# A two-layer Mamba and MLP block on one core: scan tiles of 16 channels by 8 states instead of 8 by 16

## The chip, the cores and the metric

The kernel runs on one core of a Trainium2 chip. The metric is the device time of one execution in microseconds, as a median of runs. The profile page shows one profiled execution; its engines are PE (matmul), PEld (weight load), DVE (VectorE), ACT (ScalarE), POOL (GpSimd), and SP, which here only issues DMAs.

## The reference, cut to what matters

Input x is (8 images, 64, 64, 96) in float32. Layer 0 is a visual state-space block. Per image, after group normalisation and a projection, a depthwise 3x3 convolution and SiLU give u, 192 channels by L = 4096 positions. Four scans (k = 0..3) run over it: row order, column order, and both reversed.

```python
dts, Bs, Cs = split(x_proj_w[k] @ u_k)          # 6, 16 and 16 rows, each L long
delta = softplus(dt_proj_w[k] @ dts + dt_proj_b[k])
def step(h, inp):                               # h: (192 channels, 16 states)
    ul, dl, Bl, Cl = inp
    dA = exp(dl[..., None] * A)
    h = dA * h + (dl * ul)[..., None] * Bl[:, :, None, :]
    y = einsum('bkdn,bkn->bkd', h, Cl)
    return (h, y)
```

The four results are summed in row-major order, normalised, gated with SiLU(z), projected back to 96 channels and added to x. Layer 1 upsamples by two with a band-limited filter, applies a 96-384-96 MLP with a quadratic activation, filters, downsamples and adds.

## The kernel before

**The main stream.** For each image the four directions run in the order k = 1, 0, 2, 3, and each in NCH = 4 chunks of T = 1024 positions. A chunk has NT = 24 tiles of 128 partitions by 1024 positions: 8 channels by 16 states each. The program is written as one loop over all 3072 tiles (8 x 4 x 4 x 24, L1207). In step i it places, on in-order engines:

- `fetch` of tile i + 6 (L1070): SP issues one DMA that broadcasts 8 rows of du = delta * u from DRAM over the 16 states, 512 KB, into one of 4 buffers `dub`;
- `product_c` of tile i - 1 if that tile belongs to POOL (every third one, `by_pool`);
- `product_b` of tile i + 3 (L1078): POOL multiplies dub by `br`, the broadcast of B, into one of 4 buffers `bb`;
- `decay` of tile i + 1 (L1082): six bf16 matmuls on PE copy delta (in three bf16 parts) to the 128 partitions, and ACT applies exp with the scale `neg_a`;
- `scan` of tile i (L1097) on DVE, then `product_c` by `cr`, the broadcast of C, on DVE unless the tile is POOL's, and `hold` (L1118), which keeps the last column in `carry`;
- `sums` (L1132), every second step: matmuls with `sel_r` add the 16 states of a channel.

`LEAD, FETCH = 3, 6` (L1184) are the distances. For each chunk `prepare` (L956) loads u, projects it to xd (rows for delta, C and B), broadcasts B and C from SBUF in halves of 256 KB, and computes delta and du, which goes to DRAM in 6 transfers. POOL multiplies delta by u there (L1040). It runs about one chunk ahead.

**The side work.** Everything else is cut into generators that yield what the next piece needs of each engine. `Side.advance` (L109) runs once a step: each active generator moves one piece if the allowance per step (`CAPS`, L50) has it. `front` (L516) of the next image does normalisation, convolution and the gate z. There `conv` (L573) computes blocks of 8 columns and ACT copies each, transposed, into `xt` (L592), which holds the whole image; `lay` (L601) writes it to DRAM in row order once all blocks are done, in rows of 2 KB per channel or pieces of 128 bytes. `tail` (L648) of the image before loads the sum of the row-order directions as a whole table `ye` (L657), then per block of 8 columns loads `ty` (column-order sum) and `tz` (gate); POOL adds (L687), PE, ACT and DVE normalise, gate and project. `mlp` (L783) is layer 1, with `up_h`, `rows_` and `down_h`; its tiles `t1s`, `t1r`, `xu`, `mq` rotate in few buffers. SP issues all transfers on one queue, in the order of the program, and stands when an earlier one must wait for its buffer or its data.

After the last tile the last image's tail and MLP are drained with nothing beside them.

Of the kernel before, what the change touches and what calls it, by code (L numbers as in the profile page):

```python
# [18 lines left out]
HF = 2  # L19
Q3 = 3  # L20
NS = 16
R = 6
K = 4
# [15 lines left out]
class Side:  # L39
# [10 lines left out]
    CAPS = dict(pe=(2.5, 3.2), act=(2.3, 3.0), dve=(1.5, 1.5), pool=(1.4, 2.7), dma=(270, 450))  # L50
# [87 lines left out]
def kernel(ctx: ExitStack, tc: tile.TileContext, a: dict, out: bass.AP):  # L138
# [32 lines left out]
    for p in range(2):  # L171
# [21 lines left out]
    neg_a = cp.tile([128, K, NT], F32, name="neg_a")  # L193
    queue().dma_start(
        neg_a.rearrange("p k g -> p (k g)"),
        a["a_logs"].rearrange("(c n) k f q j -> n c (k f q j)", n=NS),
    )

    sel_r = cp.tile([128, 4, 32], F32, name="sel_r")
    queue().dma_start(  # L200
        sel_r.rearrange("p j m -> p (j m)"), a["sel_r"].rearrange("(c n) j m -> n c (j m)", n=NS)
    )

    sel_b = cp.tile([128, 8, NS, 8], BF16, name="sel_b")
# [68 lines left out]
    def constants_in():  # L273
        nc.gpsimd.memset(xp, 0.0)
        raw["sel"] = tile_([128, 8, 128], "sel_0")
# [20 lines left out]
    def constants_of_scans():  # L296
        yield {}

        nc.scalar.activation(neg_a, neg_a, AF.Exp)
        nc.vector.tensor_scalar(neg_a, neg_a, -1.0, None, ALU.mult)  # L300
        nc.vector.tensor_copy(sel_b, raw["sel"].rearrange("p j (c n) -> p j n c", n=NS))
# [214 lines left out]
    def front(b):  # L516
# [6 lines left out]
        def begin():  # L523
# [6 lines left out]
            v["xt"] = [bp.tile([128, H, w], F32, tag=f"xt{w}", name=f"xt{w}", bufs=1) for w in (W, W // 2)]  # L530
# [3 lines left out]
        def piece(g):  # L534
# [3 lines left out]
            t = bp.tile([128, 4, C], F32, tag="x", name="x", bufs=4)  # L538
# [34 lines left out]
        def conv(n, g):  # L573
# [5 lines left out]
            for tap in range(9):  # L579
# [11 lines left out]
            xt = v["xt"][n]  # L591
            nc.scalar.copy(  # L592
                xt[:, :, 8 * g : 8 * g + 8].rearrange("p h w -> p w h"), e.rearrange("p (i j) -> p i j", i=8)
            )
            for rows, cs, blk in parts_of(n, g):
                filtered.add((b, n, blk))
                nc.sync.dma_start(
                    u_dram[b][1][cs, MB * blk : MB * blk + MB], e[rows]
                )

        def lay(n):  # L601

            yield {}
            while not all((b, n, blk) in filtered for blk in range(8)):
                yield {}
            for h0 in range(0, H, 8):
                yield dict(dma=262 if n == 0 else 131)
                h1 = h0 + 8
                if n == 0:
                    src = v["xt"][0][:, h0:h1].rearrange("p h w -> p (h w)")  # L610
                    nc.sync.dma_start(u_dram[b][0][0:128, W * h0 : W * h1], src)
                else:
                    u = u_dram[b][0][128:192].rearrange("c (h w) -> c h w", h=H)
                    for p in range(2):
                        nc.sync.dma_start(u[:, h0:h1, 32 * p : 32 * p + 32], v["xt"][1][64 * p : 64 * p + 64, h0:h1])
            yield {}
            laid.add((b, n))
# [21 lines left out]
        lays = [(4, 0, lambda n=n: lay(n)) for n in range(2)]  # L639
# [4 lines left out]
        if b == 0:  # L644
            return start + convs[:4], convs[4:] + lays + gates + [bp.close(), bp.close()]
        return start, convs + lays + gates + [bp.close()]

    def tail(b, keep, pairs=True):  # L648
# [3 lines left out]
        def begin():  # L652
# [4 lines left out]
            v["ye"] = [bp.tile([C, H, W], F32, tag=f"ye{f}", name=f"ye{f}", bufs=1) for f in range(HF)]  # L657
            for h0 in range(0, H, 8):
                for f in range(HF):
                    yield dict(dma=200)  # L660
                    nc.sync.dma_start(
                        v["ye"][f][:, h0 : h0 + 8].rearrange("p h w -> p (h w)"),
                        y_dram[b][0][f * C : f * C + C, W * h0 : W * h0 + 8 * W],
                    )
            yield {}
            yield {}

        def block(g):
# [6 lines left out]
            for t, src in zip(yz, (y_dram[b][1], z_dram[b])):  # L675
                for f in range(HF):
# [3 lines left out]
                    )  # L680
# [686 lines left out]
```

## Time and profile before

| | |
|---|---|
| median of 3 runs | 10,879.19 us (10,876.58 to 10,884.08) |
| profiled execution, its own time | 10,889.88 us |
| span in the profile, granted PE clock | 10,888.1 us, 0.977 |
| first scan starts, last scan ends | 139.2 us, 10,612.8 us |
| POOL: products by B / by C / u | 7183.5 / 2423.0 / 491.7 us |
| DVE: scans (four groups) / products by C | 7159.9 / 2508.7 us |

The page gives the busy time of each engine and, for groups of instructions, what ended the idle time ahead of them. Durations overlap by some tens of ns where instructions follow each other, so work per tile is read from one start to the next.

### The profile page before, as it was taken

Reading aid. Unit: us, or ns where it says so; the run is one execution under the profiler, and the core shown is the slowest. Engines: PE = TensorE matmul, PEld = TensorE weight load, DVE = VectorE, ACT = ScalarE, POOL = GpSimd, SP = SyncE. Lnnn points to the kernel's source line nnn. Section 1 sums busy time; section 2 is a strip of 40 time slices with the busy share of each in tenths; the row PEclk is TensorE's granted clock in tenths of the full one; section 3 lists DMA queues with packets and bytes.
Section 4 is the critical chain, followed back from the end, with each engine's and each line's share of the span. In section 5 each row is a group of like instructions: output and inputs, shape, how many; then the busy total and the mean of one; then the engine's idle time right before and its main releaser. Section 6 shows DMA issues by size and latency. Waiting matters only on the chain. (4 is left out here: it accounts for less than half of the span.)

```text
span 10888.1 us, 152912 instructions
## 1 busy us (share of the span) xinstructions
PE 9406.6 (86%) x52498; PEld 3129.1 (29%) x52498; DVE 9965.6 (92%) x7319; ACT 6891.4 (63%) x10138; POOL 10172.5 (93%) x4674
## 2 busy tenths in 40 slices
PE   7788778988789988899889997898978989789888
PEld 2222222422233222332223322233222432223325
DVE  5999999999999999999999999999999999999990
ACT  5666556767567665666656666566756767566653
POOL 4999999999999999999999999999999999999990
PEclk8999999999999999999999999999999999999998
DMA  6879898898988989898998989899898898988981
GB/s 155 224 200 234 218 236 216 221 235 232 239 214 225 235 233 233 214 225 232 240 228 220 230 223 247 217 225 234 231 237 218 222 232 234 239 214 223 230 207 49
DMA packets 1052725, 2402.30 MB, mean 221 GB/s; under 512 B 302012, under 2 KB 322748, under 8 KB 1051944
## 3 DMA queue, kind: packets, MB, share of 16 engines
q1 hardware_dynamic: 1050968, 2391.48, 87.0%
q8 instruction: 413, 6.77, 0.3%
q14 instruction: 368, 3.01, 0.1%
q10 hardware_dynamic: 976, 1.04, 0.0%
HBM read 1929.05 MB, written 328.73 MB: 207 GB/s over the span
## 5 line engine op out<-in xcount | busy, mean ns | idle before, releaser
L1080 POOL TENSOR_TENSOR bb<-dub,br 128x1024 f32<-128x1024 f32 x3072 | 7183.5, 2367 | 149.2 <-DMA dub<-du 95.6
L1095 ACT ACTIVATE pd<-pd,neg_a 128x1024 f32<-128x1024 f32 x3072 | 3339.4, 1087 | 3051.3 <-PE pd L1087 3026.1
L1102 DVE TENSOR_TENSOR_SCAN pd<-pd,carry,bb 128x1024 f32<-128x1024 f32 x1536 | 3605.4, 2347 | 279.3 <-ACT pd L1095 162.6
L1087 PE MATMUL pd<-dp,sel_b 64*128 64x512 bf16 x18432 | 2596.7, 385 | 1075.4 <-DVE carry L1122 686.6
L1108 DVE TENSOR_TENSOR hc<-pd,cr 128x1024 f32<-128x1024 f32 x2048 | 2508.7, 1225 | 144.8 <-PE py L1141 3.2
L1108 POOL TENSOR_TENSOR hc<-h,cr 128x1024 f32<-128x1024 f32 x1024 | 2423.0, 2366 | 180.3 <-DVE h L1102 151.4
L1102 DVE TENSOR_TENSOR_SCAN h<-pd,carry,bb 128x1024 f32<-128x1024 f32 x768 | 1797.5, 2341 | 1.7 <-ACT pd L1095 1.6
L1141 PE MATMUL py<-hc,sel_r 128*32 128x512 f32 x12288 | 1736.0, 620 | 48.6 <-POOL hc L1108 47.1
L1087 PEld LDWEIGHTS <-sel_b 64*128 64x128 bf16 x18432 | 722.7, 94 | 3602.7 <-issue 1557.1
L1102 DVE TENSOR_TENSOR_SCAN pd<-pd,bb 128x1024 f32<-128x1024 f32 x512 | 1173.3, 2292 | 128.2 <-ACT carry L1122 52.2
L565 PE MATMUL pc<-pad,convr 96*128 96x512 f32 (+1 forms) x2304 | 844.0, 610 | 2.1 <-issue 2.1
L1115 PE MATMUL idle<-xp,ident 128*128 128x384 f32 x1450 | 662.9, 540 | 3.2 <-ACT t1s L807 3.2
L1102 DVE TENSOR_TENSOR_SCAN h<-pd,bb 128x1024 f32<-128x1024 f32 x256 | 583.7, 2280 | 14.8 <-ACT pd L1095 11.6
L1040 POOL TENSOR_TENSOR u<-dl,u 128x512 f32<-128x512 f32 x384 | 491.7, 1280 | 108.7 <-ACT dl L1035 108.7
L1017 PE MATMUL pv<-xd,dt_w 64*64 64x512 f32 x1536 | 425.4, 632 | 166.9 <-ACT xd L994 164.5
L1141 PEld LDWEIGHTS py<-hc,sel_r 128*32 128x32 f32 x12288 | 253.4, 109 | 977.2 <-issue 751.4
L859 PEld LDWEIGHTS p<-w2q,mq 128*100 128x100 f32 x4800 | 461.9, 168 | 169.3 <-issue 135.2
L852 PE MATMUL ph<-xu,w 96*128 96x500 f32 x960 | 493.6, 617 | 16.0 <-ACT xu L846 9.2
L859 PE MATMUL p<-w2q,mq 128*100 128x96 f32 x4800 | 504.2, 256 | 2.3 <-ACT mq L853 2.3
L1032 PE MATMUL pv<-e,ident 128*128 128x512 f32 x768 | 437.1, 651 | 27.9 <-ACT pv L1030 27.0
L1042 ACT CAST dp<-pv 128x512 bf16<-128x512 f32 x768 | 452.1, 589 | 5.0 <-PE pv L1041 5.0
L984 PE MATMUL px<-u,xp 64*64 64x512 f32 x1536 | 417.2, 618 | 5.1 <-DMA u<-u 3.2
(162 smaller groups left out, 8195.4 us busy)
## 6 DMA issues: line engine op xcount, KB each, us to landing
dub<-du SPq DMA_DIRECT2D x3072, 512.0 KB
u<-u SPq DMA_DIRECT2D x768, 128.0 KB
du<-u SPq DMA_DIRECT2D x768, 128.0 KB
y<-yq SPq DMA_DIRECT2D x768, 128.0 KB
br<-xd SPq DMA_DIRECT2D x256, 256.0 KB
cr<-xd SPq DMA_DIRECT2D x256, 256.0 KB
yp<-y SPq DMA_DIRECT2D x384, 128.0 KB
yp<-u SPq DMA_DIRECT2D x192, 128.0 KB
```

The source lines that it names most:

```text
L565: nc.tensor.matmul(t[rows].rearrange("p (i j) -> p i j", i=8), weights[:, cs], v["pad"][:, 8 * blk + kw : 8 * blk + kw + 8, kh : kh + H], ...
L852: nc.tensor.matmul(t[:, :px], w1[:, m, :], xu, start=True, stop=True)
L859: nc.tensor.matmul(t[:SIDE, C * i : C * i + C], sq[:, m, row], w2q[:, m, :], start=(m == 0), stop=(m == 2))
L1040: nc.gpsimd.tensor_tensor(v["u"][:, q, :], dl, v["u"][:, q, :], ALU.mult)
L1042: nc.scalar.copy(dp[:, p, :], t)
L1080: nc.gpsimd.tensor_tensor(t["bb"], t["dub"], t["got"]["br"], ALU.mult)
L1087: nc.tensor.matmul(pd[:, MB * hf : MB * hf + MB], sel_b[rows, 4 * t["s"] + t["j"]].rearrange("p n c -> p (n c)"), t["got"]["dp", t["q"]][r ...
L1095: nc.scalar.activation(pd, pd, AF.Exp, scale=neg_a[:, t["k"], t["g"] : t["g"] + 1])
L1102: nc.vector.tensor_tensor_scan(t["h"][:, ::step], pd[:, ::step], t["bb"][:, ::step], 0.0 if t["first"] else held, ALU.mult, ALU.add)
L1108: (nc.gpsimd if t["by_pool"] else nc.vector).tensor_tensor(t["hc"], t["h"], t["got"]["cr"], ALU.mult)
L1115: nc.tensor.matmul(p, ident, xp[:, 0:2].rearrange("p k q r -> p (k q r)"), start=True, stop=True)
L1141: nc.tensor.matmul(py[r0 : r0 + 32], sel_r[:, t["j"], :], t["hc"][:, MB * hf : MB * hf + MB], start=(t["j"] == 0), stop=(t["j"] == 3 and t ...
```

## The change

A tile is now 16 channels by 8 states. Two tiles (i and i + 2) hold the lower and upper 8 states of the same 16 channels and share one `dub`, fetched once; `FETCH` is 7. The product by B stays one instruction per tile. B and C go to DRAM (`bc`) and come back as broadcasts of 8 states each, two for B (one tile `br` of two halves) and two for C (three rotating tiles `cr`; the second half of the next chunk's C is fetched in the last step of a chunk). `xt` becomes three rotating tiles of 16 columns, which are written out as soon as two neighbouring blocks are done, in pieces of 16 elements (64 bytes). The table `ye` is loaded per two blocks, 16 columns at a time, also in pieces of 64 bytes. Several side buffers are fewer, and the allowance of DMA per step is larger.

```diff
-    CAPS = dict(pe=(2.5, 3.2), act=(2.3, 3.0), dve=(1.5, 1.5), pool=(1.4, 2.7), dma=(270, 450))
+    CAPS = dict(pe=(2.5, 3.2), act=(2.3, 3.0), dve=(1.5, 1.5), pool=(1.4, 2.7), dma=(450, 700))
...
-    neg_a = cp.tile([128, K, NT], F32, name="neg_a")
...
+    neg_a = cp.tile([128, 2, K * NT // 2], F32, name="neg_a")
+    sel_r = cp.tile([128, 2, 32], F32, name="sel_r")
...
+    sel_b = cp.tile([128, 4, 128], BF16, name="sel_b")
...
-            t = bp.tile([128, 4, C], F32, tag="x", name="x", bufs=4)
+            t = bp.tile([128, 4, C], F32, tag="x", name="x", bufs=3)
...
-            xt = v["xt"][n]
+            two = (n, g // 2)
+            if two not in v:
+                v[two] = bp.tile([128, H, 16], F32, tag="xt", name="xt", bufs=3)
...
+            v[n, "done"] = v.get((n, "done"), ()) + (g,)
+            if g ^ 1 in v[n, "done"]:
+                side.stores.append([l := lay(n, g // 2), next(l)])
+
+        def lay(n, two):
+
+            yield {}
+            xt, u = v[n, two], u_dram[b][0].rearrange("c (h w) -> c h w", h=H)
+            for h0 in range(0, H, 16):
+                yield dict(dma=131)
+                h = slice(h0, h0 + 16)
+                for rows, cs, blk in parts_of(n, 2 * two):
+                    nc.sync.dma_start(u[cs, h, 8 * blk : 8 * blk + 16], xt[rows, h, :])
...
-            v["ye"] = [bp.tile([C, H, W], F32, tag=f"ye{f}", name=f"ye{f}", bufs=1) for f in range(HF)]
-            for h0 in range(0, H, 8):
-                for f in range(HF):
-                    yield dict(dma=200)
-                    nc.sync.dma_start(
-                        v["ye"][f][:, h0 : h0 + 8].rearrange("p h w -> p (h w)"),
-                        y_dram[b][0][f * C : f * C + C, W * h0 : W * h0 + 8 * W],
-                    )
...
+            if ("ye", g // 2) not in v:
+                ye = v["ye", g // 2] = bp.tile([C, HF, H, 16], F32, tag="ye", name="ye", bufs=2)
+                for f in range(HF):
+                    src = y_dram[b][0][f * C : f * C + C].rearrange("c (h w) -> c h w", h=H)
+                    for h0 in range(0, H, 32):
+                        yield dict(dma=200)
+                        nc.sync.dma_start(
+                            ye[:, f, h0 : h0 + 32, :], src[:, h0 : h0 + 32, 16 * (g // 2) : 16 * (g // 2) + 16]
+                        )
...
-                s.append(bp.tile([SIDE, MB], F32, tag="t1s", name="t1s", bufs=5))
+                s.append(bp.tile([SIDE, MB], F32, tag="t1s", name="t1s", bufs=4))
...
-            s = v[r0] = bp.tile([128, 5, C], F32, tag="t1r", name="t1r", bufs=4)
+            s = v[r0] = bp.tile([128, 5, C], F32, tag="t1r", name="t1r", bufs=3)
...
-            xu = bp.tile([C, px], F32, tag="xu", name="xu", bufs=4)
+            xu = bp.tile([C, px], F32, tag="xu", name="xu", bufs=3)
...
-                    sq = bp.tile([128, 3, px], F32, tag="mq", name="mq", bufs=3)
+                sq.append(bp.tile([128, px], F32, tag="mq", name="mq", bufs=6))
...
+    def repeat(got, name, half):
+
+        if name == "cr":
+            t = got[name, half] = pp.tile([128, T], F32, tag=name, name=name, bufs=3)
+        else:
+            if half == 0:
+                got[name] = pp.tile([128, 2, T], F32, tag=name, name=name)
+            t = got[name][:, half, :]
+        r0 = NS * (name == "br") + 8 * half
+        nc.sync.dma_start(t, got["bc"][None, r0 : r0 + 8, :].to_broadcast([NS, 8, T]))
...
-            for name, row in (("br", 48), ("cr", 32)):
-                t = got[name] = pp.tile([128, T], F32, tag=name, name=name)
-                for hf in range(2):
-                    yield dict(dma=256)
-                    src = xd[64 * hf + row : 64 * hf + row + NS, None, :]
-                    nc.sync.dma_start(t[:, MB * hf : MB * hf + MB], src.to_broadcast([NS, 8, MB]))
+            bc = got["bc"] = dr.tile([2 * NS, T], F32, tag="bc", name="bc")
+            yield dict(dma=128)
+            for hf in range(2):
+                nc.sync.dma_start(bc[:, MB * hf : MB * hf + MB], v["xd"][64 * hf + 32 : 64 * hf + 64, :])
+            yield {}
+            yield {}
+            for name, half in (("br", 0), ("br", 1), ("cr", 0), ("cr", 1))[: 4 if first else 3]:
+                yield dict(dma=512)
+                repeat(got, name, half)
...
-    def fetch(t):
-        assert t["got"].get("ready", 0) > t["q"]
-        t["dub"] = sp.tile([128, T], F32, tag="dub", name="dub", bufs=4)
-        g = t["g"]
-        nc.sync.dma_start(
-            t["dub"], t["got"]["du"][None, 8 * g : 8 * g + 8, :].to_broadcast([NS, 8, T])
-        )
+    def fetch(m):
+
+        t = tiles[m]
+        assert t["half"] == 0 and t["got"].get("ready", 0) > t["q"]
+        t["dub"] = tiles[m + 2]["dub"] = sp.tile([128, T], F32, tag="dub", name="dub", bufs=4)
+        r0 = 64 * t["q"] + 32 * t["s"] + 8 * t["j"]
+        nc.sync.dma_start(t["dub"], t["got"]["du"][r0 : r0 + 16, None, :].to_broadcast([16, 8, T]))
...
-        nc.gpsimd.tensor_tensor(t["bb"], t["dub"], t["got"]["br"], ALU.mult)
+        nc.gpsimd.tensor_tensor(t["bb"], t["dub"], t["got"]["br"][:, t["half"], :], ALU.mult)
+
+    def fetches(i):
+
+        if i % 4 < 2 and 0 <= i < len(tiles):
+            fetch(i)
...
-    LEAD, FETCH = 3, 6
+    LEAD, FETCH = 3, 7
...
-            if i + FETCH < n:
-                fetch(tiles[i + FETCH])
+            fetches(i + FETCH)
+            if i % NT == NT - 1 and i + 1 < n:
+                repeat(tiles[i + 1]["got"], "cr", 1)
```

## The prediction

> **What bounds the kernel now.** I read the page first: its busy line, the DMA line and the costliest groups.
>
> ```profile
> span 10888.1 us, 152912 instructions
> PE 9406.6 (86%) x52498; PEld 3129.1 (29%) x52498; DVE 9965.6 (92%) x7319; ACT 6891.4 (63%) x10138; POOL 10172.5 (93%) x4674
> DMA packets 1052725, 2402.30 MB, mean 221 GB/s; under 512 B 302012, under 2 KB 322748, under 8 KB 1051944
> q1 hardware_dynamic: 1050968, 2391.48, 87.0%
> L1080 POOL TENSOR_TENSOR bb<-dub,br 128x1024 f32<-128x1024 f32 x3072 | 7183.5, 2367 | 149.2 <-DMA dub<-du 95.6
> L1102 DVE TENSOR_TENSOR_SCAN pd<-pd,carry,bb 128x1024 f32<-128x1024 f32 x1536 | 3605.4, 2347 | 279.3 <-ACT pd L1095 162.6
> L1108 POOL TENSOR_TENSOR hc<-h,cr 128x1024 f32<-128x1024 f32 x1024 | 2423.0, 2366 | 180.3 <-DVE h L1102 151.4
> ```
>
> POOL and DVE are both full, and the DMA engines are not far behind. How full the two are per tile is in the timeline of each, start to start (three products in a row are one line of the first view):
>
> ```profile
> 5012.47 1.26 POOL L1040 TENSOR_TENSOR u<-dl,u 128x512 f32<-128x512 f32 x1
> 5013.70 4.67 POOL L1080 TENSOR_TENSOR bb<-dub,br 128x1024 f32<-128x1024 f32 x2
> 5018.33 2.34 POOL L1108 TENSOR_TENSOR hc<-h,cr 128x1024 f32<-128x1024 f32 x1
> ...
> 5000.41 2.35 DVE L1102 TENSOR_TENSOR_SCAN pd<-pd,carry,bb 128x1024 f32<-128x1024 f32 x1
> 5003.94 2.34 DVE L1102 TENSOR_TENSOR_SCAN h<-pd,carry,bb 128x1024 f32<-128x1024 f32 x1
> 5006.36 2.36 DVE L1102 TENSOR_TENSOR_SCAN pd<-pd,carry,bb 128x1024 f32<-128x1024 f32 x1
> ```
>
> A POOL product is (5018.33 - 5013.70) / 2 = 2.31 us, a u product 1.23. A chunk of 24 tiles has 24 products by B, 8 by C and 3 u products: 32 x 2.31 + 3 x 1.23 = 77.6 us. On DVE a scan with its product by C takes 5003.94 - 5000.41 = 3.53 us and a scan for POOL 2.42, so three tiles take 9.48 and a chunk 75.8. Everything else in a chunk can add to the time only by waits, or by side work on these two engines. The windows of four chunks of one image (us, busy per engine, PE clock, DMA share, GB/s):
>
> ```profile
> 5442.00:5529.80 87.80, 70.46 (x342) 18.08 (x334) 79.47 (x63) 48.83 (x74) 84.94 (x40) 1.00 1.02 249
> 5704.60:5792.70 88.10, 71.80 (x398) 21.70 (x390) 78.43 (x64) 51.28 (x81) 79.04 (x38) 0.87 0.79 210
> 5949.40:6026.30 76.90, 73.89 (x489) 31.46 (x488) 74.21 (x41) 56.36 (x80) 76.90 (x36) 1.00 0.90 223
> 6184.70:6265.00 80.30, 68.30 (x416) 24.86 (x412) 78.06 (x62) 51.00 (x81) 74.79 (x34) 1.00 0.99 243
> ```
>
> The third runs at POOL's own 77 us although DMA is 90% busy: loaded DMA engines alone cost nothing. The others lose time. The chain of waits names what for:
>
> ```profile
> POOL hc L1108 <- DVE h L1102: 151.4, 160, 7.3
> DVE pd L1102 <- ACT pd L1095: 202.8, 246, 2.8
> DVE pd L1102 <- ACT carry L1122: 119.1, 148, 3.7
> POOL bb L1080 <- DMA dub<-du: 95.6, 86, 6.1
> DVE pd L1102 <- POOL bb L1080: 72.3, 32, 25.3
> ACT t1s L807 <- DMA t<-t1s: 68.2, 51, 4.3
> SPq L1074 <- POOL bb L1080: 3636.4, 1861, 7.0
> ```
>
> Of POOL's waits only 95.6 us are for a broadcast of du that has not landed (89.5 of them after the first chunk). The last line is why: SP stands a third of the time before a fetch whose buffer POOL still reads, so a fetch leaves three tiles ahead of its use, and all other transfers stand behind it.
>
> **The change, part by part.**
>
> *Broadcasts of du.* 3072 DMAs of 512 KB become 1536. The packet records by size give 393,344 packets of 4 KB with a mean of 258 ns, 6340 us on each of 16 engines; half, 3170, goes. B and C take 512 DMAs of 512 KB where there were 512 of 256 KB: 65,536 packets at 258 for 123 ns (the 2 KB mean), +552 us; the detour of B and C through DRAM adds 8192 packets of 2 KB, +63. In the built order the buffer of the fetch of tiles 8 and 10 is free after the product of tile 2, so a fetch now leaves five products (5 x 3.3 = 16.5 us) ahead of its use in place of three (10 us). The longest wait of before was 6.1 us, so the wait on dub goes: between 0 and -95.6 us. Where DVE is the fuller engine the time doesn't come back whole (the fourth window: POOL loses 5.5 us, but DVE has 78.06 busy), and 89.5 is the part in the loop. I take -80, near the upper end, since in the waiting chunks both engines show holes.
>
> *Engines.* Products, scans, exponentials and matmuls keep number and shape; PE loads one of 4 selections where there were 8. 0 us. Start to start, POOL's product is 2.314 us with DMA under 30% busy and 2.313 at over 90%, so a lighter DMA doesn't quicken it.
>
> *Side work earlier.* The table of even rows, 16 transfers ahead of the tail, is no longer loaded up front, and the DMA allowance per tile rises from 270 to 450. In the built order the tail's first addition on POOL stands at tile 401 of the stream where it stood at 420 (image 1 starts at 384), and DVE's side work of a chunk is more bunched (3 and 9 gates in two chunks where it was 8 and 4; 4, 4, 4 convolutions where it was 2, 4, 4, 2). With 0.70 us for each DVE piece and 1.5 for each addition, the sum over 128 chunks of the larger of 75.8 + DVE's and 77.6 + POOL's is 10,224 us before and 10,248 after: +24. Bounds: 0, as three tiles of lead smooth it, and +48.
>
> *Pieces of 64 bytes.* Laying out u takes 393,216 stores of 64 bytes, where it had 65,536 of 128 bytes and 8192 of 2 KB; reading the even rows takes 393,216 loads where it had 12,288 of 2 KB. The nearest rows: 64-byte loads of constants took 10.4 ns each, 128-byte stores 13.4, 384-byte ones 31.5 in the mean. By the first the new pieces cost 511 us of the engines, by the last 1549, for 213 removed. The queue's 87.0% (9473 us) becomes (9473 - 3170 + 552 + 63 - 213 + 511) / 10888 = 66%, or 76%. That hides them in the mean, not in a burst: two blocks issue 8 loads of 3072 pieces in four tiles (13.4 us), twice per image. At 10.4 ns one is 3072 x 10.4 / 16 = 2.0 us and the eight 16; with 2 fetches (4.1) and other loads (some 5) the backlog is 25 - 13.4 = 12 us, under the 16.5 of the lead: 0. At 31.5 ns one is 6.0, the backlog 44 us and the wait 27 us, 16 times: +430. I take 0, as the 64-byte row is the same size and direction. POOL's addition of the even rows now waits on these loads, three pauses (10 us) behind the last issue; behind it stand the products by B. The same backlog covers it.
>
> The Trainium skill ("DMA: Bandwidth & Descriptors", Specifications) speaks against these pieces: it asks for at least 512 bytes for line rate and says that below it the engine reads, modifies and writes. No run here shows what that costs at 64 bytes; the 10.4 and 13.4 ns above show no jump. If it did make a piece as dear as the 384-byte row, the sum would be the +430 case.
>
> *Smaller buffers.* t1s 4 for 5, t1r 3 for 4, xu 3 for 4, mq 6 for 9, x 3 for 4, xt in three parts. The copy to t1s already waits 68.2 us for its transfer; a buffer less adds, the freer queue takes off. Bounds: -32 us (what DVE and POOL lost behind it) and +32; 0. The order of the last image's MLP on PE is unchanged, so its 240 us of PE in the last 288 us stay.
>
> *Ends.* In the last image the even rows of the last two blocks are now fetched behind their other loads. POOL waited 9.0 us there for ty; four more issues (0.6 each) and 4 x 2.0 us come on top of it: between +4 (overlapping issue) and +26 (6.0 each); I take +7. At the start, writing B and C out and reading them back, and 5 more issues of constants, lie beside the convolutions (PE is busy from 68.8 to 110 us, while SP idles): +3, between 0 and +8.
>
> Sum: -80 + 24 + 0 + 0 + 7 + 3 = -46. The profiled execution took 10,889.9 us (span 10,888.1); it lies 10.7 above the median of 10,879.2. So 10,843.9 against the profile, **10,833** as a median.
>
> **The rivals.** A difference under 0.2% (22 us: 10,857 to 10,901) is about what a measurement cannot tell from none.
>
> 1. *The small pieces clog the queue (slower).* The place is the burst of 8 loads at the start of each image. It decides above some 13 ns per piece, where the backlog passes the lead. For it: 384-byte pieces cost 31.5, and the fastest burst of 128-byte stores (1024 in 1.18 us on 16 engines) makes 18.5 each. Against it: the constants at 10.4. At 18.5 one load is 3.55 us, the backlog 24, less 16.5: 8 us, 16 times, +128: 10,833 + 128 + 8 in the tail = 10,969.
> 2. *The waits only change their name (same).* DVE is as full as POOL; its waits for ACT and POOL's for DVE (322 and 151 us) don't come from DMA. If half of the 80 comes back: 10,873.
> 3. *The freer queue does more.* The ACT wait for t1s goes too (-32), and bunching costs nothing (-24): 10,777; with 32 of DVE's 72.3 us of waits for POOL's product gone as well, 10,745.
>
> **How the numbers follow.** Forecast (10,780 to 10,857): 0.52. Rival 1: 0.22. Rival 2: 0.16. Rival 3: 0.10. Faster is the forecast and rival 3, 0.62; same 0.16; slower 0.22. The range goes from 10,745 to 10,940: it leaves out the dearer part of rival 1 (0.12) and little below. Faster cases alone: 10,745 to 10,857.
>
> **What would show it.** Right: POOL's wait for dub falls from 95.6 to under 15 us, SP's wait for POOL to a small part of 3636, q1 at 64 to 70%, products still 2.31 us apart, the chunk with DMA waits 3 to 5 us shorter. Wrong: dub or the even rows still named behind POOL's idle time, a DMA share near 1 at the start of each image, q1 above 76%; or POOL's and DVE's waits for each other and for ACT growing by as much as dub's shrink.

## The result

The changed kernel took 10,895.63 us (median, 10,879.09 to 10,906.54) beside 10,879.46 us (10,863.63 to 10,906.51) for the kernel before, run beside it. The ratio is 1.0014, with a 95% interval of 1.0007 to 1.0020: 15 us, or 0.14%, slower. By the bound of 0.2% that is "the same"; the forecast was 46 us faster.

The page of the changed kernel, with the rows that answer to those of before (busy line, DMA line, queue, and three groups with busy time, mean ns, and idle time by releaser):

```profile
span 10896.6 us, 149147 instructions
PE 9467.0 (87%) x52574; PEld 3148.1 (29%) x52574; DVE 9965.9 (91%) x7319; ACT 6875.2 (63%) x10139; POOL 10172.9 (93%) x4674
DMA packets 1545527, 1747.69 MB, mean 160 GB/s; under 512 B 1003868, under 2 KB 1024476, under 8 KB 1544776
q1 hardware_dynamic: 1543800, 1737.14, 67.0%
L1100 POOL TENSOR_TENSOR bb<-dub,br 128x1024 f32<-128x1024 f32 x3072 | 7179.2, 2365 | 65.0 <-DVE pd L1131 49.8 <-DMA dub<-du 10.1 <-DVE h L1131 1.9
L1137 POOL TENSOR_TENSOR hc<-h,cr 128x1024 f32<-128x1024 f32 x1024 | 2420.4, 2364 | 236.4 <-DVE h L1131 176.1 <-PE px L1004 33.1 <-PE pd L1116 9.9
```

The queue fell from 87.0% to 67.0%, as worked out (66%). POOL's wait for dub fell from 95.6 to 10.1 us. POOL is as busy as before and the time did not fall, so POOL lost elsewhere what it gained here. The waits of the whole run (total, times, longest) show where, the last two lines for SP's queue:

```profile
POOL hc L1137 <- DVE h L1131: 176.1, 179, 6.5
DVE pd L1131 <- ACT pd L1124: 163.2, 232, 2.1
DVE pd L1131 <- ACT carry L1151: 123.2, 155, 6.4
POOL bb L1100 <- DVE pd L1131: 49.8, 77, 2.3
POOL ty L696 <- DMA ye<-y: 34.0, 5, 20.8
SPq L1096 <- POOL bb L1100: 2250.2, 894, 12.2
SPq L1066 <- POOL u L1062: 1284.1, 347, 13.3
```

POOL waits 25 us longer for DVE's h (151.4 before), and 34 us for the even rows, which had no wait on this list; 22.9 of the 34 are in the end. The last row of the page names a third place: 33.1 us put down to PE's px, the projection of a later chunk. Before, that was

```profile
POOL hc L1108 <- PE px L984: 9.2, 7, 1.8
```

DVE's wait for ACT's exponentials, in contrast, fell from 202.8 to 163.2 us. SP still stands 3534 us for POOL; the second line is the store of du behind the u product.

I cut the profiled time into three parts, from DVE's timeline: the start (up to the first scan), the loop (first scan's start to the last scan's end), and the end (from there to the end of the span). Parts in this document are cut so, one profiled execution each. Such an execution can lie well off the median of its kernel (10.7 us above it for the kernel before, 17 below it for the sharing alone further down), so differences under some 20 us are not resolved by the parts.

| | start | loop | end |
|---|---|---|---|
| before | 139.2 | 10,473.6 | 275.3 |
| changed | 141.2 | 10,456.9 | 298.5 |
| difference | +2 | -17 | +23 |

So the loop gained 17 us where 56 (80 less 24) were forecast, and the end lost 23 where 7 were. The rest of this part is the search for both.

### The profile page after: what moved, and what is told of

Same layout as the page of the kernel before. It is cut to its first block, busy times and chain, and to the rows that moved or that the text cites. A ratio compares the mean times of both kernels' runs of the same rounds, so it can differ in the third digit from the quotient of the medians.

```text
span 10896.6 us, 149147 instructions
## 1 busy us (share of the span) xinstructions
PE 9467.0 (87%) x52574; PEld 3148.1 (29%) x52574; DVE 9965.9 (91%) x7319; ACT 6875.2 (63%) x10139; POOL 10172.9 (93%) x4674
## 5 line engine op out<-in xcount | busy, mean ns | idle before, releaser
L1144 PE MATMUL idle<-xp,ident 128*128 128x384 f32 x1526 | 698.0, 540 | 21.6 <-ACT t1s L816 16.2
```

Of the source, the lines that this page charges most:

```text
L1144: nc.tensor.matmul(p, ident, xp[:, 0:2].rearrange("p k q r -> p (k q r)"), start=True, stop=True)
```

## The experiments

**The side half alone.** The change has two halves: tiles that share a broadcast of du, and a side half (even rows, laying out of u, smaller buffers, larger allowance) that makes the room for them. The side half was put on the kernel before, once with a fifth dub buffer.

```diff
 kernel before, with
+ CAPS dma=(450, 700), lay() by 16 columns, ye by 16 columns, t1s 4, t1r 3, xu 3, mq 6, x 3
 and in the second run
-        t["dub"] = sp.tile([128, T], F32, tag="dub", name="dub", bufs=4)
+        t["dub"] = sp.tile([128, T], F32, tag="dub", name="dub", bufs=5)
```

> The kernel before with only the side half of the change: xt, lay and ye by 16 columns in 64-byte pieces, fewer side buffers, the larger DMA allowance; tiles, fetches and broadcasts of B and C as before. Theory A (DVE is as full as POOL, so the waits for dub were nearly free, and the end of the program pays for the late even rows): about +23 us of tail and a loop within 20 us of the kernel before, 10,885 to 10,925. Theory B (the dub waits were worth some 80 us, and the side half gives them back inside the loop): the loop some 60 us longer as well, 10,945 to 10,980. In both POOL still waits for dub, 60 to 130 us.

> The same with a fifth dub buffer, so that a fetch no longer stands behind POOL; the traffic stays as before. POOL's wait for dub should fall under 20 us. Theory A: within 25 us of the side half alone, with POOL's wait for DVE higher by 20 us or more. Theory B: 60 to 90 us under the side half alone.

Measured: 11,324.89 us, ratio 1.0411 (1.0397 to 1.0425), and with the fifth buffer 11,288.85, ratio 1.0378 (1.0364 to 1.0393). The first lies 345 us above its expectation. The second was put relative to the first: its 36 us lie between the two theories, and POOL's wait for dub is 465 us, not under 20. From the page of the first:

```profile
span 11311.2 us, 153087 instructions
q1 hardware_dynamic: 1752408, 2391.48, 87.8%
L1081 POOL TENSOR_TENSOR bb<-dub,br 128x1024 f32<-128x1024 f32 x3072 | 7184.1, 2364 | 594.4 <-DMA dub<-du 527.0
```

POOL waits 527 us for dub, not 95.6, while the queue's share is 87.8% of a longer span (87.0% before). The windows of one image (us, busy of PE, PEld, DVE, ACT, POOL, PE clock, DMA share, GB/s) say when; the first line is chunk 0 of the kernel before, the others are chunks 0 to 2 of this run:

```profile
4051.10:4128.00 76.90, 59.93 (x318) 16.02 (x314) 73.78 (x57) 42.10 (x59) 76.64 (x35) 0.98 0.93 230
4179.90:4285.70 105.80, 74.73 (x328) 19.13 (x328) 77.47 (x61) 47.12 (x70) 83.72 (x40) 0.86 1.02 205
4285.70:4378.20 92.50, 74.92 (x423) 21.94 (x421) 83.80 (x69) 52.06 (x80) 84.30 (x40) 0.96 0.97 206
4378.20:4478.50 100.30, 82.08 (x461) 25.73 (x460) 86.62 (x74) 54.06 (x83) 91.75 (x44) 0.94 0.89 216
```

Chunk 0, where the even rows are now read, takes 105.8 us at a DMA share of 1.02, where it took 76.9 at 0.93 before. The DMA engines are full there, and a deeper dub (465 us of waits in place of 527) does not change that. The two kinds of 64-byte pieces apart, each on the kernel before; the run of the even rows has the smaller side buffers and the larger allowance in it:

> The kernel before with the new reading of the even rows (64-byte loads, two blocks at a time, allowance 450/700 for transfers) and the smaller side buffers, but the old laying out of u. The side half as a whole costs 447 us while the broadcasts of du stay unshared. Theory of the pieces (393,216 loads of 64 bytes and as many stores, on DMA engines that are already 95% busy): in the run of the side half, chunks 0 to 4 of an image, where the even rows are read, are 35 us longer than before and chunks 9 to 14, where u is laid out, 19; so some 250 to 300 us here, 11,125 to 11,180, chunk 0 over 100 us in place of 76.8, chunks 12 and 13 as before (81.8 and 84.2). Rival (reads and writes only clog the queue when they come together, or the larger allowance lets everything go at once): below 11,000 with chunk 0 under 85, or above 11,280 with chunks 9 to 14 longer too.

> The kernel before with the new laying out of u alone (393,216 stores of 64 bytes in pieces of 16 columns; the allowance for transfers stays 270/450), the old reading of the even rows. Theory of the pieces: chunks 9 to 14 of an image grow as in the run of the side half (12.3 us in chunk 13, 6.4 in chunk 12, 19 in sum), chunks 0 to 4 stay: some 100 to 170 us, 10,980 to 11,050. Rival (the larger allowance makes the bursts, not the size of the pieces): under 10,920, with chunk 13 within 3 us of 84.2.

Measured: even rows 11,208.18 us, ratio 1.0289 (1.0273 to 1.0304), chunk 0 at 104.6 us in the mean of six images (all but the first and the last) and chunks 12 and 13 at 83.2 and 82.0; laying out 10,996.47, ratio 1.0103 (1.0089 to 1.0116), chunks 12 to 14 at 84.1, 90.1 and 92.5 and chunks 0 to 4 as before. 315 + 112 make 427 of the 447. Both are dear with a full queue, each in the chunks where it falls. The even rows cost 28 us more than the range expected; these 315 us are not the pieces alone, as order, allowance and buffers go with them. Laying out u was inside its range, with the old allowance, so its loss does not need the larger one.

**The sharing alone.** In the kernel before, one fetch serves tiles i and i + 2. This kernel, and those below that build on it, leave out half of the channels' own du: tile i + 2 multiplies by that of tile i. They serve for the time alone.

```diff
-        t["dub"] = sp.tile([128, T], F32, tag="dub", name="dub", bufs=4)
+        t["dub"] = tiles[t["n"] + 2]["dub"] = sp.tile([128, T], F32, tag="dub", name="dub", bufs=4)
...
-    LEAD, FETCH = 3, 6
+    LEAD, FETCH = 3, 7
...
-            if i + FETCH < n:
+            if i + FETCH < n and (i + FETCH) % 4 < 2:
```

> The kernel before with one broadcast of du fetched for tiles i and i+2, so that half of its traffic and of its fetches go, and nothing else: tiles, side work, even rows and buffers stay. It leaves out half of the channels' own du (tile i+2 multiplies by that of tile i); every instruction on POOL, DVE, ACT and PE stays. It asks what the waits for dub are worth without the new side work. Theory A (where POOL waits for dub, DVE is full, so the time does not come back): the waits for dub fall under 10 us, the loop shrinks by 0 to 25 us from 10,473.6, the time is 10,852 to 10,880. Theory B, the forecast's -80 (the waits were worth nearly all of their 95.6 us, and the new side half takes them back): 10,790 to 10,815. A queue share of 60 to 63% by both (87.0% less 3170 us of 10,888, i.e. 58%, or somewhat over).

Measured: 10,826.29 us, ratio 0.9941 (0.9929 to 0.9954), so 64 us faster; loop 10,396.3, 77 less than before. That lies between the two theories and nearer to the forecast's 80. Its profiled execution is the fastest of the five, 17 us under their median, so the 77 are rather too many. The sharing does pay: between two thirds and four fifths of the 95.6 us of waits for dub came back. On this base the parts of the side half were added one by one:

```diff
 sharing alone, with
+ lay() by 16 columns, x 3                                         (laying out)
 or
+ ye by 16 columns, t1s 4, t1r 3, xu 3, mq 6, x 3, CAPS dma=(450, 700)   (even rows)
 or the last with
+ CAPS dma=(270, 450)                                              (even rows, paced)
 or
+ the whole side half
```

> Shared broadcasts on the kernel before, and the new laying out of u by 64-byte stores alone; old reading of the even rows, allowance 270/450. It leaves out half of the channels' own du. Theory of the even rows: the stores are spread and hidden once the queue is at some 65%, the loop is within 12 us of 10,396, the time 10,815 to 10,845, although the same stores cost 110 us without the sharing. Rival (laying out u takes the gain back): loop 10,430 or more, chunks 12 to 14 longer by 5 us in sum (81.8 + 83.6 + 85.1).

> Shared broadcasts on the kernel before (as in the run with sharing on the old side, 10,826 us, loop 10,396.3), and the new reading of the even rows by 64-byte loads with the allowance 450/700; old laying out of u. It leaves out half of the channels' own du. Theory of the even rows (they take back what the sharing gave): the loop is 10,440 to 10,470, chunks 0 to 2 of an image are 10 us or more longer in sum than with sharing alone (76.7 + 85.0 + 88.4), the end is 20 us longer, the time 10,880 to 10,915. Rival (laying out u, or the new tiles themselves, take it): loop within 12 us of 10,396, time 10,835 to 10,860 with the end.

> The same as shared broadcasts with the new reading of the even rows, but with the old allowance of 270/450 for transfers, so that the loads and all other side work are handed out as slowly as before. It leaves out half of the channels' own du. If the cost lies in the order of the side work that the larger allowance brings (POOL's and DVE's pieces piled into chunks 0 to 2), the loop comes back to 10,396 to 10,420. If it lies in the 64-byte loads (DMA engines held), the loop stays at 10,440 or more.

> Shared broadcasts on the kernel before, with the whole new side half (even rows, laying out, smaller buffers, 450/700). It leaves out half of the channels' own du. What it lacks of the changed kernel is B and C by halves over DRAM and the selections of 16 channels. If those cost nothing, it is the changed kernel: loop 10,445 to 10,470, end 20 us longer, 10,880 to 10,905. If B's and C's doubled traffic and detour take part of the gain, it is faster than the changed kernel by that part: loop 10,396 to 10,440.

| on sharing alone | time, us | ratio to before (interval) | loop | end |
|---|---|---|---|---|
| nothing more | 10,826.29 | 0.9941 (0.9929 to 0.9954) | 10,396.3 | 270.9 |
| laying out | 10,817.62 | 0.9946 (0.9933 to 0.9960) | 10,398.9 | 277.8 |
| even rows | 10,878.48 | 1.0001 (0.9992 to 1.0010) | 10,440.0 | 293.4 |
| even rows, paced | 10,867.55 | 0.9992 (0.9983 to 1.0001) | 10,433.7 | 291.4 |
| whole side half | 10,882.40 | 1.0003 (0.9994 to 1.0012) | 10,450.0 | 292.1 |

With half the traffic gone, the 64-byte stores of u cost nothing that can be measured, although they cost 112 us without it. The reading of the even rows, with the smaller side buffers and the larger allowance that go with it, takes the whole gain back: 44 us of the loop and 23 of the end (its total fell 2 us under the range expected). The allowance is a small part of it on this base: pacing it as before returned 6 us of the loop (10 of the whole by the ratios), which lies between the two expectations. With the whole side half the sharing is within 13 us of the changed kernel (12 by the ratios, whose intervals overlap), so the tiles of 16 channels with B and C over DRAM cost about that or less.

**Pieces or order.** The new reading both makes small loads and shifts when POOL and DVE do the tail's work. To tell these apart the same loads were made to read the same number of bytes in rows of 2 KB, once on sharing with even rows, once on the changed kernel; no instruction moves. These two fetch the wrong even rows and serve for the time alone.

```diff
-                            ye[:, f, h0 : h0 + 32, :], src[:, h0 : h0 + 32, 16 * (g // 2) : 16 * (g // 2) + 16]
+                            ye[:, f, h0 : h0 + 32, :].rearrange("c h w -> c (h w)"),
+                            src[:, 16 * (g // 2) + h0 // 4 : 16 * (g // 2) + h0 // 4 + 8, :].rearrange("c h w -> c (h w)"),
```

> The run with shared broadcasts and the new reading of the even rows (10,878 us, loop 10,440.0, end 293.4), with each of its loads reading the same number of bytes from consecutive addresses, 2 KB at a time, in place of 64-byte pieces. The order of all instructions stays. It leaves out half of the channels' own du, and adds the wrong even rows. Theory of the order (the loads are early enough, what costs is that POOL's and DVE's side work falls otherwise): the loop stays at 10,428 to 10,442, only the end comes back to 270 to 276, the time is 10,850 to 10,865. Theory of the pieces (the 64-byte loads hold the DMA engines in chunks 0 to 2): the loop comes back to 10,395 to 10,410, chunk 0 to below 78 us from 84.6, the time to 10,815 to 10,835.

> The changed kernel (10,896 us, loop 10,456.9, end 298.4), with the loads of the even rows reading the same number of bytes from consecutive addresses, 2 KB at a time. The order of all instructions stays; it adds the wrong even rows. Theory of the order: loop 10,445 to 10,458, end 270 to 280, time 10,865 to 10,880. Theory of the pieces: loop 10,405 to 10,420, chunk 0 below 78 us from 82.1, time 10,820 to 10,845.

Measured: 10,845.47 us, ratio 0.9963 (0.9950 to 0.9977), loop 10,418.7, end 288.6; and 10,867.42, ratio 0.9985 (0.9976 to 0.9993), loop 10,437.0, end 288.4. Neither theory has it alone: both loops end between the two expectations, 21 and 20 us lower than with the pieces, about half way; by the ratios the pieces are worth 41 us (0.38%, from 1.0001 to 0.9963) and 32 us (from 1.0014 to 0.9985), ends included. The rest stays with rows of 2 KB, 24 us by the ratios (0.9963 less 0.9941), the end's 18 (288.6 less 270.9) among them. It holds all that came with the new reading except the pieces: the order of the side work, the larger allowance and the smaller side buffers. How much of it is loop is not settled: the parts say 22 us, counted from an execution of sharing alone that lies 17 us under its median; the ratios leave 6. The smaller buffers were not tried alone; the wait by which they should show, ACT's t1s for its transfer, fell from 53.4 to 30.1 us.

The packet records also tell loads and stores of 64 bytes apart. With the even rows alone on sharing 396,288 pieces, all but 3072 of them the even rows' loads, took 14.2 ns in the mean; with laying out alone as many, all but 3072 of them stores, took 10.6. The median is 11 ns in both, so a small part of the pieces, which took much longer, makes the difference.

The windows of chunk 0 and chunk 1 of one image, and the sum over chunks 0 to 4: first sharing alone, then with even rows in rows of 2 KB, then in pieces of 64 bytes.

```profile
4035.50:4112.40 76.90, 59.70 (x318) 15.90 (x314) 73.78 (x57) 42.10 (x59) 76.60 (x36) 0.98 0.75 174
4112.40:4197.30 84.90, 68.13 (x342) 17.84 (x334) 79.47 (x64) 48.96 (x74) 84.90 (x40) 1.00 0.74 174
...
sum 421.00, PE 344.35 PEld 101.67 DVE 399.80 ACT 245.76 POOL 415.01; mean PE 68.87 PEld 20.34 DVE 79.96 ACT 49.15 POOL 83.00
```

```profile
4043.40:4126.10 82.70, 67.06 (x327) 17.57 (x320) 76.87 (x62) 47.41 (x70) 82.70 (x39) 0.98 0.85 201
4126.10:4214.50 88.40, 74.84 (x435) 21.90 (x435) 83.56 (x68) 51.58 (x78) 88.40 (x43) 0.96 0.65 157
...
sum 424.30, PE 363.84 PEld 117.27 DVE 399.99 ACT 259.36 POOL 414.27; mean PE 72.77 PEld 23.45 DVE 80.00 ACT 51.87 POOL 82.85
```

```profile
4051.80:4138.00 86.20, 70.21 (x327) 18.09 (x320) 76.98 (x61) 47.38 (x70) 82.21 (x39) 0.94 0.92 170
4138.00:4227.10 89.10, 74.52 (x435) 22.03 (x435) 83.71 (x69) 51.53 (x79) 89.07 (x43) 0.96 0.88 167
...
sum 427.70, PE 365.64 PEld 118.58 DVE 400.10 ACT 259.30 POOL 414.63; mean PE 73.13 PEld 23.72 DVE 80.02 ACT 51.86 POOL 82.93
```

POOL has 415 us of work in these five chunks in all three, but they take 421.0, 424.3 and 427.7 us: 3.3 for the order and what goes with it, 3.4 for the pieces. That is one image; the means of the seven are 421.0, 425.1 and 427.5. From the first to the second POOL is full through chunks 0 and 1 and then idle for 10.0 us in chunks 2 to 4, where it was 5.7. From the second to the third chunk 0 has 4 us of idle POOL at a DMA share of 0.92. The waits of the whole run name both; again sharing alone, 2 KB, 64 bytes:

```profile
POOL hc L1109 <- DVE h L1103: 169.9, 182, 7.6
DVE pd L1103 <- ACT pd L1096: 150.4, 212, 2.6
POOL bb L1081 <- DMA dub<-du: 5.9, 1, 5.9
```

```profile
DVE pd L1104 <- ACT pd L1097: 206.2, 252, 3.6
POOL hc L1110 <- DVE h L1104: 192.6, 237, 6.5
POOL ty L688 <- DMA ye<-y: 18.3, 2, 17.4
POOL bb L1082 <- DMA dub<-du: 6.0, 1, 6.0
```

```profile
DVE pd L1103 <- ACT pd L1096: 204.1, 264, 3.6
POOL hc L1109 <- DVE h L1103: 184.7, 227, 6.5
POOL ty L687 <- DMA ye<-y: 32.3, 8, 20.7
POOL bb L1081 <- DMA dub<-du: 23.7, 15, 6.0
```

The order shows as waits between engines (DVE for ACT's exponentials +56 us, POOL for DVE's h +23), the pieces as waits for transfers (dub +18, even rows +14), which is the burst of the prediction's first rival in small. In the changed kernel the wait for the exponentials is 163.2 us, so there the first of these signs is missing.

**The end and the start of the tail.** Two runs of the changed kernel: the even rows of the last image loaded as soon as their buffer is free, ahead of the block's other loads; and the tail begun 19 pauses later in the other images.

```diff
+            while not pairs and g < 4 and v.get(("added", g // 2 + 2), 0) < 2:
+                yield {}
+            if not pairs:
+                yield from even_rows(g // 2)
...
 and, in the other run alone
+            + [pause(19)] * pairs
```

> The changed kernel, with the even rows of the last image loaded as soon as a buffer is free instead of behind ty and tz; nothing else is moved. If the late even rows are what lengthened the tail, the tail falls from 298 us to 270 to 283 and the time to 10,870 to 10,882. If the tail is longer for another reason (fewer MLP buffers), it stays above 290 and the time above 10,888.

> The changed kernel with 19 pauses ahead of the first block of the tail in all images but the last, so that the side work stands about where it stood in the kernel before (first addition on POOL at tile 416 instead of 401; before 420). If the earlier, bunched side work costs time (estimate 24 us from the sum of the fuller engine per chunk, 7 of which this variant gives back), it is 5 to 25 us under the changed kernel's 10,895. If bunching costs nothing, within 5 us.

Measured: 10,875.82 us, ratio 0.9995 (0.9987 to 1.0004), end 282.7, loop 10,459.3; and 10,898.18, ratio 1.0023 (1.0013 to 1.0032), loop 10,466.0. The first recovers 16 of the end's 23 us. The timeline at the end (start, us, SP's issues and POOL's additions), first the kernel before, its first addition alone, then the changed kernel:

```profile
10623.73 1.51 POOL L687 TENSOR_TENSOR ty<-ty,ye 96x512 f32<-96x512 f32 x1 [8.56 <-DMA ty<-y]
...
10607.31 2.53 SPq L677 DMA_DIRECT2D ty<-y  x4
10609.88 1.83 SPq L677 DMA_DIRECT2D tz<-z  x4
10611.76 8.97 SPq L686 DMA_DIRECT2D ye<-y  x4
10621.41 1.51 POOL L696 TENSOR_TENSOR ty<-ty,ye 96x512 f32<-96x512 f32 x1 [20.83 <-DMA ye<-y]
```

and with the changed kernel's loads in rows of 2 KB:

```profile
10588.91 1.84 SPq L677 DMA_DIRECT2D tz<-z  x4
10590.79 1.83 SPq L686 DMA_DIRECT2D ye<-y  x4
10597.41 5.93 POOL L697 TENSOR_TENSOR ty<-ty,ye 96x512 f32<-96x512 f32 x4 [17.75 <-DMA ye<-y]
```

The four loads of 3072 pieces hold SP for 8.97 us, four of as many bytes in 2 KB rows for 1.83. That holds for loads issued back to back as here (the first of the four took 0.43, the second 4.11); over the whole run the median issue of such a load is 0.59 us. Rows of 2 KB take 10 us off the end (288.4), loading ahead 16, so the place behind eight other loads counts beside the pieces.

The second run came out as expected if bunching costs nothing, within 3 us of the changed kernel: chunk 0 comes back from 82.1 to 76.8 us (mean of six images), but chunks 3 and 4 take 91.4 and 87.5 in place of 83.6 and 83.0. Either the bunching of the tail is free, or a later start only moves its cost; this run doesn't tell which.

**Is DVE the other bound?** In the run with the even rows loaded ahead, all copies of the carry went from DVE to ACT.

```diff
-        (nc.scalar.copy if t["by_pool"] else nc.vector.tensor_copy)(
+        nc.scalar.copy(
```

> The changed kernel with the even rows of the last image loaded as soon as their buffer is free, and all copies of the carry on ACT: 1536 copies of 148 ns, 228 us, leave DVE. Theory A (DVE is as full as POOL, so waits taken from POOL come back as waits for DVE): the loop, 10,459 with the even rows loaded early, shrinks by 30 to 100 us, POOL's wait for DVE's h falls from 176, the time is 10,780 to 10,850. Rival (POOL alone bounds the loop and DVE only fills the time): within 15 us of 10,876. A third way: PE gets the buffers of pd back later, as the copy stands behind the exponentials on ACT, and DVE's wait for pd grows by more than the copies cost: above 10,890.

Measured: 11,074.97 us, ratio 1.0172 (1.0158 to 1.0186): the third way. Waits of this run:

```profile
ACT carry L1159 <- DVE hc L1145: 1390.2, 1292, 7.0
PE pd L1124 <- ACT carry L1159: 799.2, 728, 6.9
```

A copy of 148 ns that moves to another in-order engine stands there between the exponentials, and PE gets its buffers back later. Whether a lighter DVE would help stays open.

**The old even rows back in the changed kernel.** The old table needs 16 KB more per partition than the new buffers, so buffers had to go: first dub 3, hc 3 and yp 1; then dub 3, tz 2 and yp 1 with hc at 4; then that with the old allowance.

```diff
+            v["ye"] = [bp.tile([C, H, W], F32, tag=f"ye{f}", name=f"ye{f}", bufs=1) for f in range(HF)]
...
+        t["dub"] = tiles[m + 2]["dub"] = sp.tile([128, T], F32, tag="dub", name="dub", bufs=3)
 and hc 3, yp 1
 or tz 2, yp 1
 or tz 2, yp 1, CAPS dma=(270, 450), a broadcast of B or C counted as 256
```

> The changed kernel with the old table of even rows, loaded in 16 transfers of whole rows ahead of the tail. To make room, dub and hc have 3 buffers each in place of 4, and yp 1 in place of 2; the allowance of 450/700 stays. If the even rows are what took the gain back, the loop is 10,400 to 10,425 and the end 270 to 280: 10,825 to 10,850, faster than both kernels. If the three smaller buffers cost more than that, or the tiles of 16 channels do: above 10,865, with POOL's waits for dub above 15 us (room for fetches) or DVE's waits for PE py above 30 (hc).

> The changed kernel with the old table of even rows again, but with hc's 4 buffers; the room comes from dub (3 in place of 4), tz (2 for 3, so two gated blocks at a time) and yp (1 for 2). If the new reading of the even rows takes the gain back, the loop is 10,400 to 10,430 from 10,456.9 and the end 270 to 282 from 298.4: 10,825 to 10,855. If the three smaller buffers matter, or the loss is in the tiles of 16 channels: loop above 10,450, time above 10,870.

> The changed kernel with the old table of even rows (dub 3, tz 2, yp 1 for room) and the old allowance of 270/450 for transfers. If the allowance is what keeps the loop at 10,467, it comes back to 10,400 to 10,430 and the time to 10,820 to 10,850, chunk 4 below 86 us from 90.7. If the tiles of 16 channels or the smaller buffers cost it, the loop stays above 10,450 and the time above 10,870.

Measured: 12,149.66 us, ratio 1.1161 (1.1146 to 1.1176); 10,889.29, ratio 1.0001 (0.9992 to 1.0010), loop 10,467.4, end 279.6; 10,979.29, ratio 1.0094 (1.0077 to 1.0110), loop 10,566.6. In all three the second branch of the expectation came out, in the first far beyond its bound. There the missing buffer of hc takes most of it (waits):

```profile
DVE hc L1137 <- PE py L1170: 1634.1, 975, 8.2
POOL hc L1137 <- PE py L1170: 674.1, 334, 7.7
```

In the other two the stall sits in chunk 4 (90.7 us, 13 of them POOL idle) and chunk 5 (99.4 us, 20 idle), where sharing on the old side has 84.5 and 78.5. In the last, chunks 0 to 4 take 415.2 us (421.1 with sharing alone), although the side buffers are the smaller ones. So the old reading with the old allowance is good for the chunks in question, and something that the fewer buffers or the late end of the tail bring costs more behind them. These runs don't separate that; what the old reading would be worth in the changed kernel without smaller buffers is open, since there is no room to try it.

**A version that beats both.** The changed kernel with the even rows of the last image loaded ahead and the old allowance.

```diff
-    CAPS = dict(pe=(2.5, 3.2), act=(2.3, 3.0), dve=(1.5, 1.5), pool=(1.4, 2.7), dma=(450, 700))
+    CAPS = dict(pe=(2.5, 3.2), act=(2.3, 3.0), dve=(1.5, 1.5), pool=(1.4, 2.7), dma=(270, 450))
...
-                yield dict(dma=512)
+                yield dict(dma=256)
```

> The changed kernel with the allowance for transfers back at 270/450 (a broadcast of B or C counted as 256, as before) and the even rows of the last image loaded as soon as their buffer is free. With sharing on the old side the slower allowance gave 6 us of the loop and the loading ahead gave 20 us in the changed kernel: loop 10,445 to 10,455, time 10,860 to 10,872. If the order that the allowance gives is the larger part of the even rows' cost in the changed kernel: loop 10,420 to 10,440, time 10,840 to 10,858. If B and C, asked for more slowly, come late: above 10,885, with waits of DVE or POOL for cr or br.

Measured: 10,855.13 us, ratio 0.9965 (0.9953 to 0.9977), which by the ratio is 38 us faster than the kernel before; loop 10,442.0, end 279.2. The time is inside the second expectation, the loop at the bound of the two. Beside loading ahead alone that is 17 us less in the loop and 33 by the ratios (0.9995 less 0.9965). So the larger allowance costs more in the changed kernel than on the old tiles (6 and 10 us).

## Why the prediction was wrong

The table sets the prediction's terms beside what the runs gave, in us. The first measured column is from the parts of the profiled executions, the second from the ratios above times 10,880.

| term | forecast | by parts | by ratios |
|---|---|---|---|
| broadcasts of du: the waits for dub | -80 | -77 in the loop | -64 |
| order of the side work, with the allowance and the smaller side buffers (0) | +24 | +22 | +24, with 18 of the end |
| 64-byte pieces, in the loop | 0 | +21 | +41, with their part of the end |
| laying out u, B and C, tiles | 0 | +17 | +14 |
| end | +7 | +23 | in the others |
| start | +3 | +2 | in the others |
| sum | -46 | +8 | +15 |

By parts: 10,396.3 - 10,473.6; 10,418.7 - 10,396.3; 10,440.0 - 10,418.7; 10,456.9 - 10,440.0. By ratios: 0.9941 - 1; 0.9963 - 0.9941; 1.0001 - 0.9963; 1.0014 - 1.0001.

- *The waits for dub.* Right in mechanism and nearly in size: -77 by the parts, -64 by the ratios.
- *The order.* Right in sign; the size is not resolved. In the step from sharing alone the loop loses between 6 and 22 us, with the smaller side buffers in it; in the changed kernel the old allowance gives 17 to 33 back. The reading behind the +24, side work bunched so that one engine and then the other is the fuller, is not shown. Its measure, the work of the fuller engine summed over the chunks, is 415.0 us in chunks 0 to 4 of sharing alone and 414.3 with rows of 2 KB; what grows is the waits. And the later start of the tail, made against the bunching, gained nothing.
- *The step that failed* is "Pieces of 64 bytes ... I take 0". It priced the even rows' loads at the 10.4 ns of the constants, which set the burst's backlog at 12 us against a lead of 16.5. The changed kernel's 789,504 packets of 64 bytes took 12.7 ns in the mean, but that mixes the kinds: stores 10.6, loads 14.2 where each was alone. The burst is of loads, and 14.2 lies above the 13 at which the rival was to decide. By the prediction's own sum it makes one load 2.7 us, the eight 21.8, the backlog 17.5 and the wait 1 us, 16 times: some 16 us. This is an estimate worked out afterwards; as a small difference of large terms it is near the measured +21 and +20 of the loop partly by luck. With their part of the end the pieces cost 32 to 41 us. "The same backlog covers it" failed too: POOL waits 11 us in the loop for the even rows themselves (34.0 less the 22.9 of the end).
- *The upper case* of that term, +430, is within 20 us of what the side half costs where the sharing is missing (447). That is a coincidence: it was worked out for the lead and the traffic of the changed kernel.
- *The pieces and the page.* Loads of 64 bytes in 14.2 ns are 4.5 bytes per ns and engine, 4 KB in 258.5 ns is 15.8. The Trainium skill ("DMA: Bandwidth & Descriptors", Specifications) asks for at least 512 bytes per piece for line rate; the runs agree in direction. They don't bear out the fear that a piece costs as much as the 384-byte row (31.5 ns).
- *The end.* Forecast +7, measured +23. The four issues were taken as 0.6 us each and took 8.97 together. The first addition starts 23.3 us after the last scan (10,621.4 less 10,598.1), where it was 11.0 (10,623.7 less 10,612.7): 12 of the 23 us. The rest falls behind it and was not followed up; with the even rows loaded ahead 7 us stay.
- *Laying out u, B and C, tiles.* Taken as 0; together +14 to +17, under the resolution of the parts. POOL's waits put down to px grow here: 33.1 us in the changed kernel, 10.5 with the whole side half on the old tiles. No run follows that up.
- *SP.* "SP's wait for POOL to a small part of 3636" was wrong: 2250 for dub and 1284 for the store of du. With fetches in pairs SP still arrives early at a buffer in use, and the next entry of the queue, behind a u product, is now the one that waits. It cost nothing that was seen, since sharing alone has the same two waits (2146.6 and 1241.6) and is 64 us faster.
- *The rivals.* The second ("waits only change their name") comes nearest in time (10,873), but its reason did not hold: on the old side the waits did not come back. The first (the small pieces clog the queue) has the right cause for about half of the miss; its price of 128 us, worked out at 18.5 ns a piece, was too high.

## What to carry over

Before a change that saves traffic in one place and spends small pieces in another is costed, price the pieces in the stretch where they are issued, at that stretch's DMA share: the same reading of the even rows cost 315 us on the kernel before and 65 with the sharing, where chunk 0 shows a share of 0.92. One row is thin ground for a price: the constants' 10.4 ns stood for loads that took 14.2. A backlog 4.5 us under the lead is not a cost of nothing; look also at what SP needs for each issue and at the place of the load in the queue, because at the end of the program nothing covers them. And when a change has two halves that need each other for room, cost each alone: here -64 and +447 stood behind a difference of 15.

## What the runs showed of the hardware

- Four loads of 3072 pieces of 64 bytes, issued back to back, held SP for 8.97 us, four of the same bytes in 2 KB rows for 1.83. Over a whole run the median issue is 0.59 and 0.58 us.
- Pieces of 64 bytes took 10.6 ns in the mean as stores and 14.2 as loads, each alone beside the shared broadcasts, with a median of 11 in both.
- Laying out u in 393,216 stores of 64 bytes cost 112 us on the kernel before, and nothing that was resolved with half the broadcasts gone. Reading the even rows in as many loads, with the order, allowance and buffers that go with it, cost 315 and 65 us.
- One buffer of 4 KB per partition fewer for hc (3 in place of 4) cost over 1,200 us: 12,149.66 against 10,889.29 for the nearest kernel that has four (it has one tz fewer instead).
